# Value products by halves of the context rows, in a fused cross-attention and expert kernel

## The chip, the cores and the metric

The kernel runs on one core of a Trainium2 chip. A core has a matrix engine (TensorE, PE in the profile, with its weight loads shown apart as PEld), a vector engine (VectorE, DVE), an engine for activation functions (ScalarE, ACT), a general one (GpSimd, POOL) and an engine that only issues transfers (SyncE, SP). Transfers can be put on queues by SyncE, ScalarE and GpSimd. The time is device microseconds for one execution, as the median of several runs; the profile is one further execution, recorded by the hardware profiler.

## The reference

Inputs are x (8 batches of 512 tokens, 256 wide), a condition vector per batch, a context of 64 rows per batch, and weights. All is float32.

```python
nx = _layer_norm(x, ln_gamma, ln_beta)
q = nx @ Wq
k = prototype_bank @ Wk            # the context
v = prototype_bank @ Wv
scores = jnp.einsum('bth,bph->btp', q, k) * H ** (-0.5)
weights = jax.nn.softmax(scores, axis=-1)
evidence = jnp.einsum('btp,bph->bth', weights, v)
anchor = jnp.broadcast_to(global_anchor[:, None, :], nx.shape)   # the condition
combined = jnp.concatenate([nx, evidence, anchor], axis=-1)
router_probs = jax.nn.softmax(combined @ router_W + router_b, axis=-1)
h = jax.nn.silu(jnp.einsum('btc,ecr->bter', combined, e_w1) + e_b1)   # 3 experts
expert_out = jnp.einsum('bter,erh->bteh', h, e_w2) + e_b2
routed = jnp.sum(expert_out * router_probs[..., None], axis=-2)
g = jax.nn.sigmoid(jax.nn.silu(combined @ gate_w1 + gate_b1) @ gate_w2 + gate_b2)
return x + g * (routed @ out_w + out_b)
```

## The kernel before

The eight batches are worked in four pairs. One long opening prepares what all pairs need and the first pair's own inputs; then a loop over the pairs runs a gate layer, three expert layers and the outputs. The instructions are written out by hand in one order, and each engine works through its own part of that order; nothing is reordered between engines but by waits on data.

The opening, from line 1200 on, is what the change touches. The context (512 rows in all) arrives in two halves of 256 rows on SyncE's queue, then Wv and the first two batches of x; Wk and Wq arrive on ScalarE's queue. `wake` (line 289) runs products of a tile of zeros on PE into a bank that nothing reads: seven ahead of the first data and one between the two context halves (each product is two instructions in the trace[...]). `context_transposes` (line 311) turns each half on PE and copies it to `ctxT`, the first half by VectorE, the second by ScalarE. `transpose_weights` (326) turns Wk and Wq. `project` (335) with Wv makes the values, 128 of their columns at a time over all 512 context rows, and `keep_v` (344) copies them. `join_keys` (347) multiplies the two weight matrices into one, so that scores can be had from the context and the normalised x without separate keys and queries; `project` with that product and `keep_m` (358) give `mr`, in which the first context row of each batch is subtracted from the others.

Beside this VectorE computes `statistics` (540) and `normalize` (553) of both batches, with the square root on ScalarE in `deviation` (550); `transpose_x` (574) turns the result on PE, and `scale_x` (564) applies scale and shift, one half of the width on VectorE and one on ScalarE. `small_transposes` (297) turns the rows of biases and the condition.

`scores` (642) multiplies, and starts the softmax on VectorE; for the first pair it subtracts the largest score on VectorE and leaves the exponential to one instruction on ScalarE. `value_weights` (762) multiplies values by expert weights, `value_differences` (782) prepares one part of the result. `softmax` (686) and `turn_weights` (692) finish the attention weights.

The first layers use a scheme with seven products in place of eight for a two-by-two block product. `combine_x` (631) makes the four differences t1 to t4 of x that it needs, in the tile T and in two parts of the second batch's x; `nx_product` (843) uses them. In the first pair's case t1 and t2 are computed ahead of `scores`, t3 behind the softmax, and t4 in the first expert layer.

PSUM banks of the opening are taken in rotation by `either` (283). The rotation is one line:

```python
        return bank((1, 2, 0, 3)[turn[0] % 4], name)
```

Of the kernel before, what the change touches and what calls it, by code (L numbers as in the profile page):

```python
# [10 lines left out]
ALU = mybir.AluOpType  # L11
# [5 lines left out]
def kernel(  # L17
# [100 lines left out]
    def load_table(func):  # L118
        nc.scalar.activation(warm_t, warm_t, func)
# [32 lines left out]
    def rows_of(w):  # L152
        return w.rearrange("(k p) n -> p k n", p=P)
# [8 lines left out]
    def by_k(flat, n):  # L162
# [14 lines left out]
    rw, rw2, m0, rw_all, gamma_all = (  # L177
        scr[:, NL : NL + 3 * KH * E].rearrange("p (k e) -> p k e", e=E),
        scr[:, NL + P : NL + P + KH * TB].rearrange("p (k e) -> p k e", e=TB),
        scr[:, NL + 2 * P : NL + 2 * P + B],  # L180
        scr[:, NL + 4 * P : NL + 4 * P + H * E].rearrange("p (d e) -> p d e", e=E),
        scr[:, NL + 4 * P + H * E : NL + 4 * P + H * E + H],
    )
# [105 lines left out]
    def wake(n):  # L289

        if not ps_wake:
            ps_wake.append(misc("ps_wake"))
        for _ in range(n):
            nc.tensor.matmul(ps_wake[0][:, :P], zeros, zeros, start=True, stop=True)  # L294


    def small_transposes():
        pt = either("pt_rows")
        nc.tensor.transpose(pt[:, :NR], rows, ident[:NR, :NR])
        nc.vector.tensor_copy(cols, pt[:, :NR])  # L300
        nc.gpsimd.tensor_copy(b2T[:, :, :E], b2_c.rearrange("p e k -> p k e"))
        pt = either("pt_cond")
        for k in range(KH):
            nc.tensor.transpose(
                pt[:, k * B : (k + 1) * B], cond_sb[:, k * P : (k + 1) * P], ident[:B, :B]
            )
        nc.vector.tensor_copy(
            condT[:, :, :B], pt[:, : KH * B].rearrange("p (k b) -> p k b", b=B)
        )

    def context_transposes():
        for d in range(2):
            if d:
                wake(1)
            pt = either(f"pt_ctx_{d}").rearrange("p (k c) -> p k c", k=KH)
            for k in range(KH):
                for t in range(NX // 2):
                    nc.tensor.transpose(
                        pt[:, k, t * P : (t + 1) * P],
                        ctx_sb[:, d * (NX // 2) + t, k * P : (k + 1) * P],  # L320
                        ident,
                    )
            half = slice(d * NX // 2 * P, (d + 1) * NX // 2 * P)
            (nc.scalar.copy if d else nc.vector.tensor_copy)(ctxT[:, :, half], pt)

    def transpose_weights(dst, w_sb, name):
        pt = either(f"pt_{name}")
# [13 lines left out]
                )  # L341
            evacuate(m, ps)

    def keep_v(m, ps):
        nc.scalar.copy(vT[:, m, :], ps)

    def join_keys():

        ps = either("ps_kq").rearrange("p (m n) -> p m n", n=H)
        for m in range(KH):  # L350
            for k in range(KH):
                nc.tensor.matmul(
                    ps[:, m, :], wkT[:, k, m * P : (m + 1) * P], wqT[:, k, :],
                    start=(k == 0), stop=(k == KH - 1),
                )
        nc.scalar.copy(wkqT, ps)

    def keep_m(m, ps):
        ps = ps.rearrange("p (b c) -> p b c", c=CT)
        nc.vector.tensor_copy(m0, ps[:, :, 0])  # L360
        nc.vector.tensor_tensor(
            mr[:, m, :, 1:], ps[:, :, 1:], m0.unsqueeze(2).to_broadcast([P, B, CT - 1]), ALU.subtract
        )


# [208 lines left out]
    def transpose_x(b):  # L574
        S["nxT", b] = npool.tile([P, KH, T], F32, tag="nxT", name=f"nxT_{b}")
        for k in range(KH):
            pt = misc(f"pt_x_{b}_{k}")
            for t in range(NT):
                nc.tensor.transpose(
                    pt[:, t * P : (t + 1) * P], S["xn", b][:, t, k * P : (k + 1) * P], ident  # L580
                )
            scale_x(S["nxT", b][:, k, :], k, pt, k % 2 == 0)

    def logits(j):

# [45 lines left out]
    def combine_x(j, engine, ts=range(4)):  # L631

        b11, b21, b12, b22 = (S["nxT", 2 * j + i][:, k, :] for i in range(2) for k in range(KH))
        if 0 in ts:
            S["T", j] = work.tile([P, 3, T], F32, tag="T", name=f"T_{j}", bufs=1)
        t1, t2, t4 = (S["T", j][:, i, :] for i in range(3))
        t3 = b12
        for i, (dst, p, q) in enumerate(((t1, b12, b11), (t2, b22, t1), (t3, b22, b12), (t4, b21, t2))):
            if i in ts:
                engine.tensor_tensor(dst, p, q, ALU.subtract)  # L640

    def scores(j):


        ps = misc(f"ps_s_{j}")
        for g in range(2):
            for k in range(KH):
                for i, h in SIDES:
                    nc.tensor.matmul(  # L649
                        ps[side(i, h), g * NH : (g + 1) * NH],  # L650
                        mr[:, k, 2 * j + i, g * TB : (g + 1) * TB],
                        S["nxT", 2 * j + i][:, k, h * NH : (h + 1) * NH],
                        start=(k == 0),
                        stop=(k == KH - 1),
                    )
        w = work.tile([P, 2, NJ, TB], F32, tag="w", name=f"w_{j}", bufs=1)
        S["w", j] = w
        tokens = w.rearrange("p g j c -> p j g c")
        nc.vector.transpose(w.rearrange("p g j c -> p (g j c)"), ps)
        nc.vector.tensor_copy(logits(j)[:, 1, :], w[:, 0, :, 0])  # L660
        nc.vector.memset(w[:, 0, :, 0], 0.0)
        mx = work.tile([P, NJ], F32, tag="mx", name=f"mx_{j}")
        nc.vector.tensor_reduce(mx, tokens, AX.XY, ALU.max)
        sm = work.tile([P, NJ], F32, tag="sm", name=f"sm_{j}")
        S["sm", j] = sm
        if j == 0:
            nc.vector.tensor_tensor(w, w, by_token(mx), ALU.subtract)
            nc.scalar.activation(w, w, AF.Exp, scale=SCALE)
            return
        nmx = work.tile([P, NJ], F32, tag="nmx", name=f"nmx_{j}")  # L670
        nc.vector.tensor_scalar_mul(nmx, mx, -SCALE)
        for t in range(NJ):
            nc.scalar.activation(
                w[:, :, t, :], w[:, :, t, :], AF.Exp, bias=nmx[:, t : t + 1], scale=SCALE,
                accum_out=sm[:, t : t + 1],
            )
# [6 lines left out]
    def by_token(a):  # L683
        return a.unsqueeze(1).unsqueeze(3).to_broadcast([P, 2, NJ, TB])
# [158 lines left out]
    def nx_product(j, n, which, start=False):  # L843
        q = GROUPS[n]
        c = 2 * q
        A, Bx, T_ = S["nxT", 2 * j], S["nxT", 2 * j + 1], S["T", j]

        def a(k, d):
            return w1[:, k, (c + d) * P : (c + d + 1) * P]

        dst, lhsT, rhs = {
            1: (U, a(0, 0), A[:, 0, :]),
            2: (Y, a(1, 0), A[:, 1, :]),
            3: (Z, ws[:, S4, q, :], Bx[:, 1, :]),
            4: (U, a(1, 1), T_[:, 2, :]),
            5: (Z, ws[:, S1, q, :], T_[:, 0, :]),
            6: (U, ws[:, S2, q, :], T_[:, 1, :]),
            7: (U, a(0, 1), Bx[:, 0, :]),
        }[which]
        product(dst[n], lhsT, rhs, start=start)  # L860

# [337 lines left out]

    with tc.manual_schedule(engines=None):  # L1200
        ctx_rows = context.flatten_outer_dims().rearrange("(t p) d -> p t d", p=P)
        for d in range(2):
            half = slice(d * NX // 2, (d + 1) * NX // 2)
            nc.sync.dma_start(ctx_sb[:, half, :], ctx_rows[:, half, :])
        for w_sb, w in ((wk_sb, Wk), (wq_sb, Wq)):
            nc.scalar.dma_start(w_sb, rows_of(w))
        nc.sync.dma_start(wv_sb, rows_of(Wv))
        load_table(AF.Sqrt)
        load_x(0)
        load_x(1)  # L1210
# [4 lines left out]
            load_first(g)  # L1215

        wake(7)
        context_transposes()
        transpose_weights(wkT, wk_sb, "wk")
        transpose_weights(wqT, wq_sb, "wq")  # L1220
        statistics(0, 0, NT)
        deviation(0, 0)
        normalize(0)
        project(wv_sb, ctxT, keep_v, "v", (0,))
        join_keys()
        project(wv_sb, ctxT, keep_v, "v", (1,))
        statistics(1, 0, NT // 2)
        small_transposes()
        statistics(1, NT // 2, NT)
        transpose_x(0)  # L1230
        deviation(0, 1)
        load_router_column()
        normalize(1)
        load_table(AF.Exp)
        project(wkqT, ctxT, keep_m, "m")
        router_anchor()
        transpose_x(1)
        value_weights(0, E)
        store_router_rows(0)
        store_router_anchor()  # L1240
        combine_weights(E)
        combine_x(0, nc.vector, (0, 1))
        scores(0)
        router_column()
        spread_router_bias()
        combine_weights(0)
        spread_router_rows(0)
        value_weights(0, 0, nc.scalar.copy, False)
        anchor_rows(E)
        anchor_rows(0)  # L1250
        sum_weights(0)
        softmax(0)
        value_differences(0, 0)
        combine_x(0, nc.vector, (2,))
        turn_weights(0)
        late_scratch()
        load_anchor(1)
# [123 lines left out]
```

## Time and profile before

| | us |
|---|---|
| median of 3 runs | 462.98 (462.89 to 463.24) |
| the profiled execution | 463.12 |
| its span, first to last instruction | 461.3 |
| PE busy in the span | 456.4 |
| VectorE busy | 365.2 |
| ScalarE busy | 214.7 |
| GpSimd busy | 100.4 |

The opening lasts until about 24.4 us, when the first gate product begins. A line of the chain gives the start, the length and the work of a piece that the end of the program hangs on. A line of the timeline gives start, length, engine, line in the kernel, operation, output and inputs, and in brackets how long the engine had been idle and what ended that. The durations of single PE instructions overlap, because they are pipelined; the distance from one start to the next tells the rate.

### The profile page before, as it was taken

What the parts mean: (1) busy time and instruction counts of PE and PEld (TensorE: products, weight loads), DVE (VectorE), ACT (ScalarE), POOL (GpSimd) and SP (SyncE); (2) the same over time, 40 slices, a digit from 0 to 9 for tenths busy, and PEclk for the clock granted to TensorE, in tenths of its full rate; (3) what the DMA queues carried; (4) which work ended last, traced back from release to release, by engine and by line L of the source; (5) the groups of instructions that cost most, each with busy time, mean ns of one, the idle gap of its engine ahead of it and who ended that gap; (6) DMA issues with size and microseconds to landing.
All of it is one profiled execution on the core that took longest, in us unless ns stands there. A gap on an engine that the chain in (4) does not pass through costs nothing.

```text
span 461.3 us, 4752 instructions
## 1 busy us (share of the span) xinstructions
PE 456.4 (99%) x1455; PEld 210.1 (46%) x1455; DVE 365.2 (79%) x683; ACT 214.7 (47%) x370; POOL 100.4 (22%) x149
## 2 busy tenths in 40 slices
PE   9999999999999999999999999999999999999996
PEld 7544555444444444444444444444444444444445
DVE  2988979969799669869799659879889625787973
ACT  3445683664222666556221576548221456457000
POOL 6357715001181200001072300001072300000020
PEclk9999999999999999999999999999999999999999
DMA  8975677302013326802012235702011570000013
GB/s 275 370 158 128 102 232 126 83 0 46 7 23 46 76 87 142 159 18 46 6 24 32 37 136 120 110 0 46 6 24 23 82 195 0 0 0 1 0 22 70
DMA packets 119401, 35.27 MB, mean 76 GB/s; under 512 B 106044, under 2 KB 116336, under 8 KB 118864
## 3 DMA queue, kind: packets, MB, share of 16 engines
q1 hardware_dynamic: 115312, 27.02, 28.9%
q0 software_dynamic: 2176, 7.17, 4.7%
q10 hardware_dynamic: 1888, 0.79, 0.6%
q8 instruction: 11, 0.18, 0.2%
q14 instruction: 14, 0.11, 0.1%
HBM read 27.56 MB, written 7.39 MB: 76 GB/s over the span
## 4 chain that ended last, share of the span: by engine, by line
PE 95%; DVE 4%; issue 0%
PE ps_u L796 43%; PE ps_z L796 18%; PE ps_y L796 14%; PE ps_vw L771 5%; PE ps_gu L796 3%; PE ps_w2o L501 2%; PE ps_s L649 2%; PE ps_gz L796 1%; DVE h L1072 1%; PE ps_tokens L796 1%; PE ps_wake L294 1%; DVE h L880 1%; PE ps_v L339 1%; PE ps_m L339 1%; PE ps_gy L796 1%; DVE r L1082 0%
## 5 line engine op out<-in xcount | busy, mean ns | idle before, releaser
L880 DVE TENSOR_TENSOR h<-h,pb 128x512 f32<-128x512 f32 x96 | 61.9, 694 | 6.5 <-ACT h L829 6.5
L796 PE MATMUL ps_u<-h,w2o 128*128 128x512 f32 x144 | 64.2, 595 | 0.0
L829 ACT ACTIVATE h<-h,abias 128x512 f32<-128x512 f32 x72 | 49.6, 719 | 13.5 <-DVE h L835 13.0
L796 PE MATMUL ps_u<-nxT,w 128*128 128x512 f32 x112 | 55.3, 604 | 0.0
L796 PE MATMUL ps_z<-wT,vw 64*128 64x512 f32 x104 | 49.5, 605 | 0.0
L1105 POOL TENSOR_TENSOR yb<-yb,xb 128x512 f32<-128x512 f32 x14 | 17.8, 1269 | 142.9 <-DVE yb L1104 138.8
L796 PE MATMUL ps_z<-h,w2s 128*128 128x512 f32 x96 | 42.6, 593 | 0.2 <-DVE r L1088 0.2
L796 PEld LDWEIGHTS ps_u<-h,w2o 128*128 128x128 f32 x144 | 27.0, 190 | 32.7 <-issue 29.4
L838 ACT COPY h<-ps_u 128x512 f32<-128x512 f32 x48 | 28.0, 582 | 29.4 <-PE ps_u L796 26.9
L415 POOL DMA_DIRECT2D vrd<-vw x8 | 5.0, 630 | 136.9 <-ACT vw L778 136.9
L1072 DVE TENSOR_TENSOR h<-h,h 128x1024 f32<-128x1024 f32 x24 | 34.3, 1483 | 0.0
L796 PEld LDWEIGHTS ps_u<-nxT,w 128*128 128x128 f32 x112 | 20.2, 189 | 29.5 <-issue 24.2
L829 ACT ACTIVATE h<-ps_u,abias 128x512 f32<-128x512 f32 x24 | 16.5, 688 | 29.7 <-PE ps_z L796 29.4
L796 PEld LDWEIGHTS ps_z<-h,w2s 128*128 128x128 f32 x96 | 18.1, 190 | 23.5 <-issue 21.8
L796 PE MATMUL ps_y<-nxT,w 128*128 128x512 f32 x56 | 28.6, 592 | 0.0
L796 PE MATMUL ps_z<-T,ws 128*128 128x512 f32 x56 | 28.6, 592 | 0.0
L835 DVE TENSOR_TENSOR h<-h,ps_y 128x512 f32<-128x512 f32 x24 | 16.4, 683 | 14.8 <-PE ps_y L796 14.0
L796 PE MATMUL ps_u<-wT,vw 64*128 64x512 f32 x56 | 27.8, 611 | 0.0
L796 PE MATMUL ps_y<-wT,vw 64*128 64x512 f32 x56 | 27.0, 596 | 0.0
L771 PE MATMUL ps_vw<-w,vT 128*128 128x512 f32 (+1 forms) x64 | 26.9, 542 | 0.0
L796 PE MATMUL ps_u<-T,ws 128*128 128x512 f32 x56 | 26.6, 592 | 0.0
L796 PE MATMUL ps_u<-T,w 128*128 128x512 f32 x56 | 26.6, 592 | 0.0
(229 smaller groups left out, 792.2 us busy)
## 6 DMA issues: line engine op xcount, KB each, us to landing
pb<-pd POOLq DMA_DIRECT2D x4, 1536.0 KB, 6.5
xb<-in_x_dram SPq DMA_DIRECT2D x64, 64.0 KB, 2.4
out_dram<-yb SPq DMA_DIRECT2D x56, 64.0 KB, 2.0
w<-in_L_xcond_e_w_dram SPq DMA_DIRECT2D x6, 512.0 KB, 10.1
x<-in_x_dram SPq DMA_DIRECT2D x24, 128.0 KB, 2.9
xd<-x SPq DMA_DIRECT2D x24, 128.0 KB, 2.4
xg<-xd SPq DMA_DIRECT2D x48, 64.0 KB, 2.4
scr_wa<-in_L_xcond_e_w_dram SPq DMA_DIRECT2D x3, 512.0 KB, 16.5
```

What stands on the lines that cost most here:

```text
L339: nc.tensor.matmul(ps, w_sb[:, k, m * P : (m + 1) * P], src[:, k, :], start=(k == 0), stop=(k == KH - 1))
L415: nc.gpsimd.dma_start(S["vrd", j][i].rearrange("e c -> c e"), S["vw", j][row_half(i), R0:])
L501: nc.tensor.matmul(ps[:, d * H : (d + 1) * H], w2T[:, k, (i + d) * P : (i + d + 1) * P], ow_sb[:, k, :], start=(k == 0), stop=(k == KH - 1),)
L649: nc.tensor.matmul(ps[side(i, h), g * NH : (g + 1) * NH], mr[:, k, 2 * j + i, g * TB : (g + 1) * TB], S["nxT", 2 * j + i][:, k, h * NH : ( ...
L771: nc.tensor.matmul(ps, vT[:, k, j * 2 * CT : (j + 1) * 2 * CT], w1[:, KH + k, n0:n1], start=(k == 0), stop=(k == KH - 1),)
L796: nc.tensor.matmul(ps, lhsT, rhs, start=start, stop=True, skip_group_check=not start)
L829: nc.scalar.activation(h, h if src is None else src, AF.Silu, bias=abias[:, c, 2 * j + i : 2 * j + i + 1])
L835: nc.vector.tensor_tensor(h, h, part, ALU.add)
L838: nc.scalar.copy(chunk(n, i, d), part)
L880: nc.vector.tensor_tensor(h, h, S["pb", j][:, i, :, 2 * q // RC, :], ALU.mult)
L1072: nc.vector.tensor_tensor(d, p, m, ALU.subtract)
L1105: nc.gpsimd.tensor_tensor(yb, yb, S["xb", 2 * j + row][:, i, :], ALU.add)
```

## The change

The context halves and Wv are each loaded in two pieces of 128 KB, one on SyncE's queue and one on ScalarE's; Wk and Wq move to SyncE's queue, behind them. Values are computed by halves of the context rows: `values(0)` as soon as the first half is turned, with three products of `wake` between, and `values(1)` ahead of `join_keys`. The two copies of a context half are shared by VectorE and ScalarE. The copy of the key product is made in two parts. The copies of the small transposes, the first column of `mr`, and the k = 0 half of the first batch's x go from VectorE to ScalarE. The products for `mr` stand around `transpose_x(0)`, and their subtractions come after the second batch is normalised. The table of the exponential is loaded later. In the first pair t3 and t4 change places, t3 is computed with t1 and t2, and the value products of the first expert and their difference are placed around the exponential.

```diff
-        scr[:, NL + 2 * P : NL + 2 * P + B],
+        scr[:, NL + 2 * P : NL + 2 * P + KH * B].rearrange("p (m b) -> p m b", b=B),
...
-        nc.vector.tensor_copy(cols, pt[:, :NR])
+        nc.scalar.copy(cols, pt[:, :NR])
...
-        nc.vector.tensor_copy(
-            condT[:, :, :B], pt[:, : KH * B].rearrange("p (k b) -> p k b", b=B)
-        )
-
-    def context_transposes():
-        for d in range(2):
-            if d:
-                wake(1)
+        nc.scalar.copy(condT[:, :, :B], pt[:, : KH * B].rearrange("p (k b) -> p k b", b=B))
+
+    def context_transposes(*ds):
+        for d in ds:
...
-            (nc.scalar.copy if d else nc.vector.tensor_copy)(ctxT[:, :, half], pt)
+            nc.vector.tensor_copy(ctxT[:, 0, half], pt[:, 0, :])
+            nc.scalar.copy(ctxT[:, 1, half], pt[:, 1, :])
...
-    def keep_v(m, ps):
-        nc.scalar.copy(vT[:, m, :], ps)
+    def values(d):
+
+        half = slice(d * NX // 2 * P, (d + 1) * NX // 2 * P)
+        ps = either(f"ps_v_{d}").rearrange("p (m c) -> p m c", m=KH)
+        for m in range(KH):
+            for k in range(KH):
+                nc.tensor.matmul(
+                    ps[:, m, :], wv_sb[:, k, m * P : (m + 1) * P], ctxT[:, k, half],
+                    start=(k == 0), stop=(k == KH - 1),
+                )
+        nc.scalar.copy(vT[:, :, half], ps)
...
-        nc.scalar.copy(wkqT, ps)
-
-    def keep_m(m, ps):
-        ps = ps.rearrange("p (b c) -> p b c", c=CT)
-        nc.vector.tensor_copy(m0, ps[:, :, 0])
+            nc.scalar.copy(wkqT[:, m, :], ps[:, m, :])
+
+    def first_column(m, ps):
+        products[m] = ps.rearrange("p (b c) -> p b c", c=CT)
+        nc.scalar.copy(m0[:, m, :], products[m][:, :, 0])
+
+    products = {}
+
+    def keep_m(m):
+        ps = products.pop(m)
         nc.vector.tensor_tensor(
-            mr[:, m, :, 1:], ps[:, :, 1:], m0.unsqueeze(2).to_broadcast([P, B, CT - 1]), ALU.subtract
+            mr[:, m, :, 1:], ps[:, :, 1:], m0[:, m, :].unsqueeze(2).to_broadcast([P, B, CT - 1]), ALU.subtract
         )
...
-            scale_x(S["nxT", b][:, k, :], k, pt, k % 2 == 0)
+            scale_x(S["nxT", b][:, k, :], k, pt, k % 2 == 0 and b > 0)
...
         t3 = b12
+        if j == 0:
+            t3, t4 = t4, t3
...
             nc.vector.tensor_tensor(w, w, by_token(mx), ALU.subtract)
+            value_weights(0, 0, nc.scalar.copy, False)
             nc.scalar.activation(w, w, AF.Exp, scale=SCALE)
+            value_differences(0, 0)
             return
...
-        for d in range(2):
-            half = slice(d * NX // 2, (d + 1) * NX // 2)
-            nc.sync.dma_start(ctx_sb[:, half, :], ctx_rows[:, half, :])
-        for w_sb, w in ((wk_sb, Wk), (wq_sb, Wq)):
-            nc.scalar.dma_start(w_sb, rows_of(w))
-        nc.sync.dma_start(wv_sb, rows_of(Wv))
+        halves = [slice(d * NX // 2, (d + 1) * NX // 2) for d in range(2)]
+        for dst, src in (
+            (ctx_sb[:, halves[0], :], ctx_rows[:, halves[0], :]),
+            (wv_sb, rows_of(Wv)),
+            (ctx_sb[:, halves[1], :], ctx_rows[:, halves[1], :]),
+        ):
+            for k, queue in enumerate((nc.sync, nc.scalar)):
+                queue.dma_start(dst[:, k : k + 1, :], src[:, k : k + 1, :])
+        nc.sync.dma_start(wk_sb, rows_of(Wk))
+        nc.sync.dma_start(wq_sb, rows_of(Wq))
...
         wake(7)
-        context_transposes()
+        context_transposes(0)
+        wake(3)
+        values(0)
+        context_transposes(1)
         transpose_weights(wkT, wk_sb, "wk")
         transpose_weights(wqT, wq_sb, "wq")
         statistics(0, 0, NT)
         deviation(0, 0)
         normalize(0)
-        project(wv_sb, ctxT, keep_v, "v", (0,))
+        values(1)
         join_keys()
-        project(wv_sb, ctxT, keep_v, "v", (1,))
         statistics(1, 0, NT // 2)
         small_transposes()
         statistics(1, NT // 2, NT)
+        project(wkqT, ctxT, first_column, "m", (0,))
+        deviation(0, 1)
         transpose_x(0)
-        deviation(0, 1)
         load_router_column()
         normalize(1)
-        load_table(AF.Exp)
-        project(wkqT, ctxT, keep_m, "m")
+        project(wkqT, ctxT, first_column, "m", (1,))
+        for m in range(KH):
+            keep_m(m)
         router_anchor()
         transpose_x(1)
         value_weights(0, E)
+        load_table(AF.Exp)
         store_router_rows(0)
         store_router_anchor()
         combine_weights(E)
-        combine_x(0, nc.vector, (0, 1))
+        combine_x(0, nc.vector, (0, 1, 2))
         scores(0)
         router_column()
         spread_router_bias()
         combine_weights(0)
         spread_router_rows(0)
-        value_weights(0, 0, nc.scalar.copy, False)
         anchor_rows(E)
         anchor_rows(0)
         sum_weights(0)
         softmax(0)
-        value_differences(0, 0)
-        combine_x(0, nc.vector, (2,))
         turn_weights(0)
```

## The prediction

> **What bounds the kernel now.** I read the page's busy shares first, then the chain of work that ended last, in order of time for the opening 33 us, then the timeline of the same stretch. The first says who is full.
>
> ```profile
> span 461.3 us, 4752 instructions
> PE 456.4 (99%) x1455; PEld 210.1 (46%) x1455; DVE 365.2 (79%) x683; ACT 214.7 (47%) x370; POOL 100.4 (22%) x149
> PE 95%; DVE 4%; issue 0%
> ```
>
> TensorE (PE) is busy 99% and holds 95% of the chain. A busy PE can hide slow or waiting matmuls, so the chain of the opening is needed. Its columns are start, length, and piece.
>
> ```profile
> 1.06 3.35 PE ps_wake L294 x14
> 4.41 1.03 PE pt_ctx L318 x4
> 5.44 0.43 PE ps_wake L294 x2
> 5.86 1.03 PE pt_ctx L318 x4
> 6.90 0.44 PE pt_wk L330 x4
> 7.33 0.44 PE pt_wq L330 x4
> 7.77 1.79 PE ps_v L339 x4
> 9.56 1.73 PE ps_kq L352 x8
> 11.28 1.72 PE ps_v L339 x4
> 13.00 0.17 PE pt_rows L299
> 13.17 0.11 PE pt_cond L304 x2
> 13.28 1.02 PE pt_x L579 x8
> 14.30 3.44 PE ps_m L339 x8
> 17.74 0.18 PE ps_rb L377 x4
> ```
>
> Two things are to be seen. Four transposes cost 1.03 us until 6.9 us and 0.44 us after it: two wakes in 0.43 us are 0.215 us each, four transposes in 0.44 us are 0.11 us each. PE works at half speed until about 6.8 us. (The granted clock in the rows of a window reads 1.00 throughout here, so the spacing must tell it.) And from 6.9 us on the pieces join: 0.22 us per 256 columns, 0.43 us per 512, apart from 0.05 to 0.15 us where a transpose follows a matmul or the reverse. The only waits for data are before 6.9 us: each pt_ctx takes 1.03 us where four at 0.215 us are 0.86 us, so 0.17 us twice, until the two context halves land at about 4.24 and 5.70 us (issue at 0.7 and 1.2 us, landing 3.5 and 4.5 us later). The timeline shows what the other engines do.
>
> ```profile
> 5.78 0.72 PEld L318 LDWEIGHTS pt_ctx<-ident,scr_ctx 128*128 128x128 f32 x4 [0.21 <-DMA scr_ctx<-in_ctx_dram]
> 8.61 0.43 DVE L547 BATCH_NORM_STATS2 st<-x 128x6 f32<-128x256 f32 x1 [2.44 <-DMA x<-in_x_dram]
> 15.92 1.38 DVE L559 TENSOR_SCALAR x<-x,mv,rstd 128x256 f32<-128x256 f32 x4
> 24.82 0.63 ACT L668 ACTIVATE w<-w 128x512 f32<-128x512 f32 x1 [4.50 <-DVE w L667]
> ```
>
> VectorE (DVE) waits for x to 8.6 us, then normalises both batches just ahead of PE; ScalarE (ACT) has gaps of microseconds. PE therefore ends when its work is done: a change before 33 us is worth only what it alters in PE's own work, in the slow stretch, or in a wait that reaches PE.
>
> **The change, PE first.** I put the after-order on the chain's clock. The 14 wakes still end at 4.41 us. First context half: four transposes at 0.215 us are 0.86 us; with the old wait 1.03 us; I take 0.95, since half the bytes now lie ahead of it but part comes over ScalarE's queue. That ends at 5.36. wake(3) in place of wake(1): six instructions at 0.215 us, 1.29 us, to 6.65. values(0): eight matmuls of 256 columns, the form of ps_kq, 1.73 us at full speed. The clock changed at 6.9 on this scale; if it does so again, 0.25 us run slowly and do 0.125 us of work, so 0.25 + 1.605 = 1.86 us, to 8.51. The second half's transposes, now at full speed, cost 0.44 us and about 0.14 us for the switch (eight pt_x take 1.02 us where 0.88 is due), to 9.09. pt_wk and pt_wq 0.88, to 9.97. values(1) 1.73 + 0.07 switch (the first ps_v is 1.79, the second 1.72), to 11.77. join_keys 1.73, to 13.50. Before, this point was 13.00: **+0.50 us**. The parts: four more wake instructions and a switch more, less the waits that fall away at half their length. Then rows, condition, m0, transpose_x(0), m1: the same pieces in another order, with one switch more, **+0.07 us**. Together +0.57 us.
>
> **Copies, with their cover.** The two ctxT copies (DVE 0.69 us, ACT 0.59 us) become four of 128x256. The nearest rows are ACT's 0.38 us for 128x258 and DVE's 0.41 us on 128x256, run side by side. The first pair ends near 6.0 us, under the wakes that last to 6.65; with no wakes PE would wait about 0.6 us there. The second pair is done near 9.7 us even behind the 0.58 us copy of values(0) on ACT, and values(1) starts at 9.97. The key product's copy becomes two of 0.38 us (0.76 for 0.59, ACT): the first lies under join_keys' second half; the second, done near 14.1 us, is wanted by m0's second half at about 14.7, and pt_rows and pt_cond lie between. Without that cover PE would wait 0.5 us. The cols and condT copies (0.15 and 0.17 us on DVE) go to ACT, where the nearest small row is 0.27 us; they are wanted at transpose_x(0)'s scaling near 16 us. first_column goes to ACT (0.16 us on DVE, 0.2 to 0.3 there). The scaling of the first x's k = 0 half goes from DVE (0.79 us) to ACT (0.78 us). ACT then has about 2 us more between 12 and 20 us, where it showed 5.5 us busy in ten.
>
> **Waits that the order adds.** DVE now has the second context copy ahead of its statistics. That copy can start when PE ends the transposes, about 9.2 us, not at 6.9; so statistics(0) starts near 9.6 us instead of 8.61. Behind it wait deviation(0,0), ACT's copy of values(1), normalize(0), and so on. Statistics and normalising of x0 took 4.2 us (8.61 to 12.79): done at 13.8, wanted at transpose_x(0) near 15.6. Statistics(1) end near 15.9 (four times 0.53, with the two small copies gone). deviation(0,1) sits on ACT behind first_column(0), which waits for m0's end at 15.5; it finishes near 16.2. normalize(1) needs 0.2 + 1.4 us, done at 17.9; transpose_x(1) wants it at about 18.6. Cover left: 0.7 us. Then the two subtractions of keep_m (0.68 us each) and the scaling of 0.80 us on DVE end near 20.2 us; scores wants them at 19.91 + 0.57 = 20.5 us. Cover left: 0.3 us. I cost both at nothing.
>
> **Loads.** ScalarE issues three pieces instead of Wk and Wq, SyncE five before x0 instead of three; at 0.46 us an issue x0 goes out near 3.1 us instead of 2.24. The bytes ahead of x0 are 1.28 MB either way, and the engines move 340 to 380 GB/s from 3 us on, so I leave x0's landing at 8.6 us. Here a rule of the Trainium skill speaks against the change: "DMA: Bandwidth & Descriptors", section "Rules for kernel authors", says that splitting a transfer or spreading it over issuing engines brings no bandwidth, since all use the same 16 engines. The row: ScalarE's Wk and SyncE's first context half, both issued at 0.74 us, landed after 3.9 and 3.5 us, sharing the engines. By the rule the first half gains only the order of its bytes: at most the 0.17 us wait, about 0.09 on the path at half speed. If the split brought the halves at twice the pace, it would be no more, because the 14 wakes end at 4.41 anyway. Both give about the same sum. Wv is wanted at 6.65, Wk at 9.1, Wq at 9.5; the old landings were 6.9 for Wv, 4.6 for Wk, 6.2 for Wq. Wv moves from behind 1 MB to behind 256 KB, so I put it near 4.7 us. Cover 1.9 us.
>
> **The softmax part.** The third difference of x, the value copy, value_differences and the Exp table are moved to where DVE or ACT had gaps; that lets wT come about 1 us earlier on DVE. PE did not wait there: its first evidence products at 31.5 us are spaced like those of the next three rounds (0.09 us over plain, each time). The gain on the path is nothing, between 0 and 0.1 us. SyncE's later loads and POOL's stores keep their order; POOL's router store waits for a copy about 0.4 us later, with over 1.5 us until PE wants its sums.
>
> **Sum.** +0.57 us, rounded to +0.5 for the possible 0.1. The profiled execution took 463.12 us: its span of 461.3 and 1.8 around it; so it becomes 463.6. The median before is 462.98, 0.14 lower; I forecast **463.5 us**, +0.11%. About 0.2%, 0.93 us, is what a measurement of this kernel can tell from no change: below 462.05 is faster, above 463.91 slower.
>
> **Rivals.** (1) *The clock comes up earlier.* For it: the slow stretch held a wait twice and eight transposes, and "TensorE: Matmul & The Clock Gate", section "Part 4: PE-mode transpose", says that transposes don't count as PE activity for the gate; now matmuls stand there. Against: four transposes came just before the change at 6.8 us and it came all the same. The same page's warm-up of 3.4 us of activity would put it at 4.5 us; the row says 5.7 us after the first wake. With 4.5, the opening from 4.4 to 6.8 us runs at double speed but waits for the copies: values(0) from about 5.5, everything 1.1 us sooner, 463.5 - 1.1 = **462.4 us**. Even that is no 0.2%.
> (2) *The late statistics reach PE (slower).* Place: DVE's copy ahead of statistics(0), through deviation(0,1) and normalize(1) to transpose_x(1) and scores. It costs PE whatever exceeds the 0.3 to 0.7 us of cover; it decides for slower at 0.4 us beyond it, thus 1.1 us of added lateness. x0 landing 1 to 2 us later behind SyncE's two more loads, or ACT's longer queue (each small copy at 0.3 us), could do it: 463.5 + 0.8 = **464.3 us**.
> (3) *The two-queue loads don't deliver.* A piece on ScalarE's queue lands late: its first packets came about 1 us after SyncE's. A late context piece costs half its lateness (slow clock), a late Wv beyond 6.65 all of it: **464.1 us** for 0.6 us.
>
> **How the numbers follow.** The likeliest case has 0.60 (its own range 463.1 to 464.0: 0.52 of it within 0.2%, 0.08 slower). Rival 1: 0.14 (0.09 same, 0.05 faster). Rival 2: 0.16 (0.13 slower, 0.03 same). Rival 3: 0.10 (0.06 slower, 0.04 same). Sums: faster 0.05, same 0.68, slower 0.27. The range leaves out a tenth on each side: 462.4, where rival 1 ends, to 464.4, just past rival 2.
>
> **What would show it.** Right: the chain is joined from 5 us on, pt_wk starts near 9.1, pt_rows near 13.5, scores near 20.5, evidence near 32.0, all about half a microsecond late, and the rest of the span is the same. Rival 1: pieces at double speed before 6 us. Rival 2: a weight load of pt_x or ps_s waiting for DVE. Rival 3: ps_v waiting for a DMA. The forecast is wrong if any wait over 0.4 us stands on PE behind 6.9 us, or if the clock steps up at another time than about 6.8 us.

## The result, and the profile after

The median went from 462.97 us (462.75 to 463.49, 22 runs) to **463.96 us** (463.31 to 466.35, 22 runs): ratio 1.0025, 95% interval 1.0019 to 1.0032. The change costs 1.0 us. The forecast was 463.5 us, in the range 462.4 to 464.4. The profiled execution took 463.63 us, 0.51 more than that of before. Nineteen of the 22 runs lie between 463.31 and 464.70. The other three (465.9 to 466.4) show a mean granted clock of 0.996 where all others show 0.999 or 1.0; 0.004 of 463 us is 1.85 us, about their excess.

The page of the changed kernel shows the busy shares as before, and one difference in the chain:

```profile
PE 455.8 (99%) x1467; PEld 210.7 (46%) x1467; DVE 364.8 (79%) x679; ACT 216.3 (47%) x377; POOL 100.6 (22%) x149
PE 93%; DVE 4%; DMA 2%; ACT 0%; issue 0%
```

PE is still 99% busy, but the chain has moved 2% from PE to a DMA. The chain of work in order of time (start, length, piece) says which:

```profile
3.40 5.46 DMA x<-in_x_dram
...
11.15 0.30 ACT sd L562
11.44 0.47 ACT vT L351
11.92 0.28 ACT scr_k L362
...
12.24 1.13 PE ps_kq L358 x4
13.38 0.17 PE pt_rows L299
...
31.97 0.62 PE ps_y L811
```

Before, the chain of this stretch was PE from end to end. Now it runs through the load of x0 (issued at 3.40 us, landed at 8.86), its statistics, and three instructions of ScalarE, and comes back to PE in the middle of `join_keys`. The timeline of the same execution shows it from PE's side (start, length, engine, line, operation; in brackets the idle time and what ended it):

```profile
4.08 0.60 PE L314 MATMUL pt_ctx<-ident,scr_ctx 128*128 128x128 f32 x4
...
4.71 0.42 DVE L320 COPY scr_ctx<-pt_ctx 128x256 f32<-128x256 f32 x1 [3.69 <-PE pt_ctx L314]
5.17 0.37 ACT L321 COPY scr_ctx<-pt_ctx 128x256 f32<-128x256 f32 x1 [1.53 <-DVE scr_ctx L320]
...
8.33 1.89 PE L347 MATMUL ps_v<-scr_ctx,scr_w 128*128 128x256 f32 x8
...
10.06 1.03 PE L358 MATMUL ps_kq<-scr_w,scr_k 128*128 128x256 f32 x4
...
12.24 1.13 PE L358 MATMUL ps_kq<-scr_w,scr_k 128*128 128x256 f32 x4 [1.16 <-ACT scr_k L362]
```

Three things are to be seen.

**A wait inside the key product.** The second four matmuls of `join_keys` could follow the first at 10.06 + 0.88 = 10.94 us. They start at 12.24, because they wait for ScalarE's copy of the first four. That copy needs only the first four, but it stands on ScalarE behind deviation(0,0), which waits for x0, and behind the copy of values(1).

**The context copies are not side by side.** ScalarE's begins at 5.17 us, when VectorE's of the same bank has ended.

The Trainium skill has a rule that would account for both, and the prediction did not look it up: "PSUM — Partial Sum Buffer", section "PSUM bank collisions raise a hardware error", says that two engines must not touch one PSUM bank (in the same quarter of partitions) at once, reads beside reads included, and that the compiler puts a dependency between any two instructions that would. The trace agrees that there is such a dependency: 0.42 us of VectorE before ScalarE starts, 1.16 us of idle PE that ScalarE's copy ends. By the rule the first part of a split copy can't lie under the second half of the product, since in the kernel both halves are parts of one bank (`ps` of `join_keys`). Who put the dependency into this program, and what would happen without it, no run here shows.

**The clock came up early.** values(1) starts at 8.33 us where the ledger had 9.97. The first four transposes, at 4.08 us, were busy for 0.60 us; in the kernel before the same four, from 4.35 us on, were busy for 1.09. So PE gained 1.6 us on the forecast's opening, and the wait in `join_keys` took it back: the pieces behind it stand at 13.38, 20.33 and 31.97 us, near the forecast's 13.5, 20.5 and 32.0. In this execution the size came out by two errors that cancel.

### The profile page after: what moved, and what is told of

The parts are those of the page before. It is cut to its first block, busy times and chain, and to the rows that moved or that the text cites. A ratio compares the mean times of both kernels' runs of the same rounds, so it can differ in the third digit from the quotient of the medians.

```text
span 461.6 us, 4784 instructions
## 1 busy us (share of the span) xinstructions
PE 455.8 (99%) x1467; PEld 210.7 (46%) x1467; DVE 364.8 (79%) x679; ACT 216.3 (47%) x377; POOL 100.6 (22%) x149
## 4 chain that ended last, share of the span: by engine, by line
PE 93%; DVE 4%; DMA 2%; ACT 0%; issue 0%
PE ps_u L811 43%; PE ps_z L811 18%; PE ps_y L811 14%; PE ps_vw L786 5%; PE ps_gu L811 3%; PE ps_w2o L512 2%; PE ps_s L662 2%; PE ps_gz L811 1%; DVE h L1090 1%; DMA x<-in_x_dram 1%; PE ps_tokens L811 1%; PE ps_m L336 1%; DVE h L898 1%; PE ps_gy L811 1%; DMA scr_ctx<-in_ctx_dram 1%; DVE r L1100 0%
## 5 line engine op out<-in xcount | busy, mean ns | idle before, releaser
L811 PE MATMUL ps_z<-nxT,ws 128*128 128x512 f32 x56 | 26.6, 592 | 0.0
```

Source lines behind the costliest of these rows:

```text
L811: nc.tensor.matmul(ps, lhsT, rhs, start=start, stop=True, skip_group_check=not start)
```

## The experiments

**The split copy, joined again (one part undone), and moved past x0 (the cause of its lateness taken away).** In the first, the key product is copied whole, after both halves. In the second the copy stays split, but deviation(0,0) and normalize(0) come behind its first part.

```diff
# e1, against the changed kernel
-            nc.scalar.copy(wkqT[:, m, :], ps[:, m, :])
+        nc.scalar.copy(wkqT, ps)
# e2, against the changed kernel
             nc.scalar.copy(wkqT[:, m, :], ps[:, m, :])
+            if m == 0:
+                deviation(0, 0)
+                normalize(0)
...
-        deviation(0, 0)
-        normalize(0)
         values(1)
```

> The changed kernel with the copy of the key product made whole again, after both halves of join_keys. Theory A (PE's second half of join_keys waits for ScalarE's copy of the first half, and that copy stands behind deviation(0,0), which waits for statistics of x): the wait of 1.3 us inside ps_kq goes; a shorter one comes ahead of the first ps_m, because the whole copy still ends near 12.5 us. PE is about 1.0 us earlier at ps_m; 463.0 us, the spread of the runs shrinks. Theory B (x normalised too late reaches PE at transpose_x(1) or scores, the copy is harmless): the wait moves there, 464.0 us as now.

> The changed kernel with the copy still in two parts, but deviation(0,0) and normalize(0) put between them, so that the first part no longer stands behind the wait for x. Theory A: the second half of join_keys still waits for the copy's own length, about 0.55 us in place of 1.3; 463.2 us. Theory B: no change or slower, 464.0 us or more, since normalize(0) is 0.25 us later.

The whole copy: 463.56 us (17 runs; 463.10 before on the same chip), ratio 1.0010 (1.0002 to 1.0017). Deviation behind the copy: 463.63 us (12 runs), 1.0011 (1.0003 to 1.0020). Against the kernel before on the same chip the changed kernel is 0.99 us longer, these two 0.46 and 0.53: either takes back about half. Both stay above the 463.0 and 463.2 us that theory A expected. The chain of the second shows what is left of the wait when ScalarE has nothing in front of the copy:

```profile
10.40 0.88 PE ps_kq L358 x4
11.30 0.38 ACT scr_k L362
11.72 1.13 PE ps_kq L358 x4
```

The eight matmuls take 2.45 us (10.40 to 12.85) where unbroken they take 1.73: a split copy costs PE 0.72 us even with ScalarE free, the copy of 0.38, its hand-over, and a slower start of PE (1.13 us for four matmuls where the first four took 0.88). The whole copy is no cure either. In its profiled execution, at 464.55 us one of its two slowest, x0 landed at 11.02 us, and PE waited one step later:

```profile
3.68 7.34 DMA x<-in_x_dram
...
14.62 1.98 PE ps_m L336 x4
```

The copy still stands behind deviation(0,0) on ScalarE (13.31 to 13.61 us here), now with the m product waiting for it.

**The split alone, in the kernel before; and x0 made later.** The first does one part of the change alone. The second loads x1 ahead of x0 in the changed kernel.

```diff
# e3, against the kernel before
-        nc.scalar.copy(wkqT, ps)
+            nc.scalar.copy(wkqT[:, m, :], ps[:, m, :])
# e4, against the changed kernel
-        load_x(0)
         load_x(1)
+        load_x(0)
```

> The kernel before with one edit: the copy of the key product in two parts. Theory A: PE stops between the halves of join_keys from about 10.3 to 12.0 us, since there too ScalarE's copy stands behind deviation(0,0), and a copy of values besides: 1.8 us slower, 464.8 us. Theory B: no change, 463.0 us.

> The changed kernel with the load of the second batch of x put ahead of the first one, so that x0 lands 512 KB later, about 1.4 us at 370 GB/s. Theory A: statistics(0), deviation(0,0) and the copy are later by the same amount, the wait inside ps_kq grows from 1.3 to about 2.7 us: 465.3 us. Theory B: the wait appears at transpose_x instead and is shorter, since statistics of both batches end at the same time: 464 to 464.5 us.

The split alone: 465.64 us (4 runs), 1.0056 (1.0041 to 1.0072). Two and a half microseconds for one line, in a kernel whose loads are as they were. x1 first: 467.10 us (4 runs), 1.0096 (1.0066 to 1.0125). Theory A expected 464.8 and 465.3 us, and the profiled executions agree: 464.88 and 465.70. What the medians have beyond that goes with the clock: two of the other runs of the first, and all three others of the second, show a mean granted clock of 0.993 to 0.996, and they are the longest. The chain of the first:

```profile
2.24 6.27 DMA x<-in_x_dram
...
11.89 1.13 PE ps_kq L352 x4
```

and of the second:

```profile
3.87 7.19 DMA x<-in_x_dram
...
14.45 1.13 PE ps_kq L358 x4
```

From the landing of x0 to the second half of the key product it is 12.24 - 8.86 = 3.38 us in the changed kernel, 11.89 - 8.51 = 3.38 here, and 14.45 - 11.06 = 3.39 with x1 first. The same distance three times, with x0 landing at three times: where the wait binds, PE's time is x0's landing plus a constant. That is shown.

**The loads: whole transfers, and the new loads alone in the kernel before.** In the first, the context halves (SyncE) and Wv (ScalarE) are one transfer each. The second keeps the kernel before, but with the change's loads. The third is the first with the whole key copy.

```diff
# e5, against the changed kernel (e7: and the edit of e1)
...
+        for queue, dst, src in (
+            (nc.sync, ctx_sb[:, halves[0], :], ctx_rows[:, halves[0], :]),
+            (nc.scalar, wv_sb, rows_of(Wv)),
+            (nc.sync, ctx_sb[:, halves[1], :], ctx_rows[:, halves[1], :]),
         ):
-            for k, queue in enumerate((nc.sync, nc.scalar)):
-                queue.dma_start(dst[:, k : k + 1, :], src[:, k : k + 1, :])
+            queue.dma_start(dst, src)
# e6, against the kernel before: the changed kernel's loads
...
-        for w_sb, w in ((wk_sb, Wk), (wq_sb, Wq)):
-            nc.scalar.dma_start(w_sb, rows_of(w))
-        nc.sync.dma_start(wv_sb, rows_of(Wv))
...
+            for k, queue in enumerate((nc.sync, nc.scalar)):
+                queue.dma_start(dst[:, k : k + 1, :], src[:, k : k + 1, :])
+        nc.sync.dma_start(wk_sb, rows_of(Wk))
+        nc.sync.dma_start(wq_sb, rows_of(Wq))
```

> The changed kernel with the same order of loads, but the context halves and Wv each as one transfer (first half on SyncE, Wv on ScalarE, second half on SyncE). Theory C (the pieces on two queues leave part of each later transfer behind: in the profiles of the changed loads the last sixteenth of x0 landed 0.6 to 2.7 us after half of it, before 0.2 us): x0 lands near 8.6 us in every execution, the runs above 465 us vanish, the wait inside ps_kq stays at about 1.2 us: 463.7 us, all runs within 0.6 us. Without C: the same median and spread as the changed kernel, 463.3 to 466.

> The kernel before with the loads of the change alone. Theory C: x0 lands 0.5 to 2.5 us later than 8.6, of which 0.4 us are covered at transpose_x(0), while the context is there 1 us sooner and helps before that: 463.3 to 465 us with a spread over 1 us. Without C: 462.7 to 463.0 us, as narrow as the kernel before.

> The changed kernel with both undone: transfers whole as in the run above, and the copy of the key product whole. Theories A and C together: no wait inside ps_kq, a short one of 0.3 to 0.5 us ahead of ps_m, no late x0: 462.9 us, all runs within 0.6 us, so level with the kernel before. If the rest of the change costs something of its own, as the prediction's sum of added wakes and switches has it, 463.4 us.

Whole loads: 464.56 us (6 runs), 1.0040 (1.0026 to 1.0055). Whole loads with the whole copy: 463.68 (16 runs), 1.0013 (1.0006 to 1.0020), level with the whole copy alone. So undoing the pieces gains nothing, and the thought that they make x0 late falls: x0 landed at 9.14 us in the first and 9.64 in the other, later than with pieces (8.86). The chain of e5 is worth showing, since in it the clock came up at about 6.4 us and PE sets the pace but for the one copy, nearly as the forecast had assumed (its key product takes 2.46 us, from 11.37 to pt_rows, against 1.73 unbroken):

```profile
6.60 1.73 PE ps_v L347 x8
...
8.77 0.44 PE pt_wk L327 x4
...
11.37 0.88 PE ps_kq L358 x4
...
13.83 0.17 PE pt_rows L299
```

And in the chain of e7 the key product is unbroken, but its whole copy has nothing to hide under: `join_keys` now comes last.

```profile
11.20 1.74 PE ps_kq L358 x8
...
13.61 1.98 PE ps_m L336 x4
```

From 12.94 to 13.61 us PE waits but for the two small transposes, which take 0.28. In the kernel before, the second product for the values stood there, 1.72 us.

The new loads in the kernel before: 463.67 us (9 runs), 1.0022 (1.0012 to 1.0031). Its chain shows a price that the change's own order of work hides: Wk, landed at 4.66 us before, lands at 7.34, and PE's first transposes of it start at 7.38 instead of 6.90.

```profile
2.12 5.22 DMA scr_w<-in_L_xcond_Wk_dram
```

That is the time which theory C expected of this run, though e5 and e7 speak against the theory's cause. In its profile x0 landed at 9.72 us, and that too reached PE, by way of VectorE, at a place that the forecast had named: `scores` starts at 20.99 us after a wait of 0.25 us for VectorE's scaling.

**The key copy with cover.** This has the whole copy, and puts half of values(1) behind `join_keys`, where the kernel before had a product too.

```diff
# e10, against the changed kernel, with the edit of e1
...
-        values(1)
+        values(1, [0])
         join_keys()
+        values(1, [1])
```

> The changed kernel with the copy of the key product whole and values(1) divided: half of its products ahead of join_keys, half behind it, so that 0.86 us of PE work lie between the key product and its use. Theory E (also a whole copy is not hidden where values(1) stands ahead of join_keys; the kernel before hid it behind its second product of values): the wait of 0.4 to 0.7 us ahead of ps_m goes, 463.1 us against 463.6 with the whole copy alone. Without E: 463.6 us.

463.39 us (13 runs; 462.97 before), 1.0006 (0.9998 to 1.0014): the lowest of the kernels with values by halves, and not told from no change. Its chain has no wait behind the key product, but a new one ahead of it:

```profile
10.15 0.50 ACT scr_w L330
...
10.69 1.99 PE ps_kq L358 x8
...
13.55 0.17 PE pt_rows L299
```

The key product needs ScalarE's two copies of the turned weights (0.59 and 0.60 us), and these stand behind its copies of values(0) and of the second context half. The whole of values(1) had covered them; half of it does not. From values(1)'s first half at 9.50 us to its second at 12.52 it is 3.02 us, where the products themselves take 0.86 + 1.73: 0.43 us are lost. The clock came up at about 6.6 us in this execution. That pt_rows stands at 13.55 us, beside the ledger's 13.50, is therefore not the ledger come true: the steps ahead of this wait ran some 0.4 us sooner than forecast, as in e5, and the wait took it back.

**The weights on ScalarE's queue.** Wk and Wq go out on ScalarE, behind its pieces, so that SyncE reaches x sooner; once in the changed kernel, once in e10.

```diff
# e9, against the changed kernel; e12, against e10
-        nc.sync.dma_start(wk_sb, rows_of(Wk))
-        nc.sync.dma_start(wq_sb, rows_of(Wq))
+        nc.scalar.dma_start(wk_sb, rows_of(Wk))
+        nc.scalar.dma_start(wq_sb, rows_of(Wq))
```

> The changed kernel with Wk and Wq back on ScalarE's queue, behind its three pieces. Theory D (what makes the end of x0's transfer late is that SyncE's queue alone carries Wk and Wq ahead of x0; the pieces have nothing to do with it): the last of x0 lands within 0.3 us of its half, near 8.5 us, the runs above 465 us vanish; the wait inside ps_kq and the clock's step remain: 463.7 us. Without D: as the changed kernel, 464.0 us with single runs near 466.

> Both edits: values(1) around join_keys with the whole copy, and Wk and Wq on ScalarE's queue. Theories D and E: 462.9 us, level with the kernel before, no run above 464. If the late context copies or the clock's step set the opening, 463.3 us.

Both missed by far: 468.35 us (4 runs), 1.0125 (1.0109 to 1.0140), and 468.24 us (5 runs), 1.0115 (1.0101 to 1.0130). The chain of e9 says why:

```profile
3.56 8.60 DMA scr_w<-in_L_xcond_Wq_dram
...
12.30 0.63 PE pt_wq L327 x4
```

Wq went out only at 3.56 us, beside both batches of x that SyncE had sent at 2.12 and 3.37, and landed at 12.16; in the changed kernel it had landed by 7.4. PE was idle 2.6 us for it. x0, sent 1.3 us sooner than in the changed kernel, landed later (9.60). In the profile of e12 the wait had a second price. A window's line gives the stretch and its length, the busy times, and, behind POOL's, the granted clock, then two figures of the DMA:

```profile
11.00:14.50 3.50, 2.02 (x7) 1.87 (x8) 0.67 (x4) 0.78 (x2) 0.96 (x6) 0.52 1.07 336
14.50:18.00 3.50, 3.50 (x9) 2.75 (x9) 3.33 (x13) 0.37 (x1) 0.00 (x0) 0.50 1.05 386
```

Within the idle stretch the clock fell, and PE ran at half speed until 18 us. In the profile of e9, with nearly the same wait, it did not (1.00 in both windows). That profile is e9's fastest run, though: its other three, and all five of e12, show a mean granted clock of 0.993 to 0.996.

**The softmax part alone, and a gentler change of the kernel before.** The first makes only the change's moves around the softmax: the third difference with the first two, t3 and t4 exchanged, the value products around the exponential. The second keeps the order of the kernel before. It loads context half 0 and Wk on SyncE and context half 1 and Wq on ScalarE, then Wv, and moves the small copies and x0's k = 0 scaling to ScalarE.

```diff
# e11, against the kernel before
+        if j == 0:
+            t3, t4 = t4, t3
...
-        combine_x(0, nc.vector, (0, 1))
+        combine_x(0, nc.vector, (0, 1, 2))
...
# e8, against the kernel before
...
-        for d in range(2):
+        for d, queue in enumerate((nc.sync, nc.scalar)):
...
-        for w_sb, w in ((wk_sb, Wk), (wq_sb, Wq)):
-            nc.scalar.dma_start(w_sb, rows_of(w))
+        nc.sync.dma_start(wk_sb, rows_of(Wk))
+        nc.scalar.dma_start(wq_sb, rows_of(Wq))
```

> The kernel before with only the part around scores and softmax: t3 with t1 and t2, t3 and t4 in each other's place, value products and their difference around the exponential. The prediction's statement that this is worth nothing on the path: 463.0 us, between -0.1 and 0; from the trace of the changed kernel, where the product with t4 starts 0.15 us later, +0.15 us: 463.2. If wT was on the path: 462.5 us.

> The kernel before with three edits: the context halves as whole transfers on two queues ahead of the weights, the small copies of cols and condT on ScalarE, and the scaling of the first x wholly on ScalarE. PE has the context about 1 us sooner, and VectorE, which feeds scores just in time, 1.1 us less to do: 462.6 us. If VectorE's feeding or the clock's step takes the gain back, 463.0 us as before.

The softmax part: 463.05 us (13 runs), 1.0001 (0.9993 to 1.0009), nothing. The gentler change: 462.82 us (13 runs; 463.03 before), 0.9997 (0.9989 to 1.0005). It is the lowest median of all, and can't be told from the kernel before. No kernel run here beats that one for certain.

## Why the prediction was right, and where it was not

The sign, the size within half a microsecond and the place (all of it in the opening) were right. The steps behind them fared unevenly, and that the number fell well inside the range is in part luck: with the stop of the copy put in, the ledger would have said +1.3 us, and in the profiled execution an early clock, which the ledger did not have, gave back what the copy took.

**The step that failed: the split copy.** "The key product's copy becomes two of 0.38 us …: the first lies under join_keys' second half." It did not; the second half waits for it. Sized by e2 and e5 that is +0.72 us where x0 is in time, which by itself takes the ledger from +0.57 to about +1.3. Where x0 is late it is whatever puts the second half at x0's landing plus 3.38 us. The prediction even said what would refute it, "any wait over 0.4 us … on PE behind 6.9 us"; there is one of 1.16 us.

**The clock.** "If it does so again" at 6.9 us: it need not. By the spacing of PE's instructions the step came at 6.8 us in the profile of before, 3.9 in the changed kernel, and anywhere from 4.0 to 7.2 us in the profiles of the experiments. Up to 3.9 us PE does the same in before and after: the same wakes. In the Trainium skill, "TensorE: Matmul & The Clock Gate", section "Part 1: The HAM clock gate", calls the window free-running, of about 3.4 us, so that the step depends on where in it the first matmul falls. The steps here spread over 3.3 us, about one such window, which agrees; that the page puts the variation at half a microsecond either way does not fit these runs. The prediction weighed that page's rule on transposes for rival 1, and not this one. Rival 1 did happen in the profiled execution, 1.6 us of it, and was swallowed by the wait.

**The loads** (landings by the last of a transfer's sixteen completion steps in the trace). The first context half landed at 3.38 us instead of 4.21. The order of bytes alone would account for most of that: the 256 KB of Wk, which came beside it before, take 0.7 us at the 340 to 380 GB/s that the prediction read (an estimate). Whether the pieces also started faster (0.41 MB had come by 3.2 us, against 0.23 before) was not tested. PE had no use for it, as forecast, since the wakes lasted to 4.1 us. Wv landed at 4.37 (forecast 4.7), Wk and Wq before they were wanted: rival 3 falls in this execution. (Its ground was misread besides: in the kernel before, ScalarE's first packets came at 2.35 us, half a microsecond after SyncE's at 1.81, not one.) x0 was put at 8.6 us and landed at 8.86 in the profile, at 9.0 to 11.0 in those of e1, e2, e5, e7 and e10. Its issue was put at 3.1 us and came at 3.40: the chain shows it waiting for the first context piece. In the kernel before, x0 left at 2.24 us.

**Rival 2** had the right mechanism, late statistics that reach PE by way of deviation, at the wrong place. It named deviation(0,1) and `transpose_x(1)`, with 0.3 to 0.7 us of cover. That cover held: the second batch's normalising ends at 17.6 us, and its transposes start at 18.36. The statistics reached PE 6 us sooner, through deviation(0,0) and the copy behind it on ScalarE.

**The rest of the ledger** stands. e5 gives its pieces one by one: values(0) at 6.60 us (forecast 6.65), pt_wk at 8.77 (9.09), join_keys at 11.37 (11.77), where about 0.13 us of the lead are the earlier clock, and most of the rest is the two switches (0.14 and 0.07 us) that the ledger charged and this chain does not show. The moves around the softmax are worth nothing (e11). One small term was missed: the first expert's product with t4 started about 0.15 us late in the profile, as VectorE's subtraction for it, 1.10 us from 35.40 on, was then still running.

**Where the 1.0 us of the medians goes.** Each kernel is taken against the kernel before on its own chip: 0.99 us for the changed kernel, 0.46 for e1, 0.65 for e7, 0.42 for e10. Joining the copy takes back about half a microsecond; that is shown. The missing cover of the whole copy (e1 and e7 against e10) comes to 0.0 to 0.2 us, no more than medians can tell here, and e10 pays for it with another wait. What is left, some 0.4 us for the added wakes and the order of work, is argued: e10's interval does not exclude nothing.

That the changed kernel's runs spread over 1.4 us where the old ones spread over 0.7 fits the same reading. The old opening waits for its second context half, which lands at 5.74 us: with the clock up at 4.2 instead of 6.8 us (the profile of e3), its first product for the values starts at 7.03 instead of 7.61. In the new order values(1) starts at 8.3 to 8.5 us with the clock up at 3.9 to 4.3 (changed kernel, e2), and at 9.6 to 9.8 with the clock up at 6.7 to 7.2 (e4, e1). That the spread of the runs comes from this is argued, not shown.

What stays open is why x0 lands late. Cutting transfers in pieces is not it (e5, e7), and sending x0 sooner is no cure (e9). The landings from the second context half on have a tail: half of a transfer's sixteen steps are in, and the last follows 0.6 to 2.7 us later for x0 (0.2 to 0.5 in before, e3 and e8).

## What to carry to other kernels

Before a copy out of PSUM is split to start earlier, ask whether the product goes on in the same bank: in this program each part was then a stop for PE (0.7 us) and not an overlap. Ask as well what stands ahead of it on its own in-order engine: a square root that waits for a load 5 us long became PE's wait. And when a product is moved, look for the copies that it used to cover: moving half of one back (e10) laid another copy bare.

## What the runs showed that was not expected

**Eight transfers at a time.** SyncE's and ScalarE's loads share eight semaphores in this program, and from the ninth on an issue waits for the earlier transfer whose semaphore it takes over. In the kernel before, the ninth load waits for Wk (what waits and for what; us in total, times, longest):

```profile
SPq L223 <- DMA scr_w<-in_L_xcond_Wk_dram: 0.8, 1, 0.8
```

Wk landed at 4.66 us and the load went out at 4.67, though the first context half had been there since 4.21. In the changed kernel the ninth load is x0, which the pieces pushed back to that place: it waits for ScalarE's first context piece (landed at 3.38, issue at 3.40). In e9 Wq is the tenth and waits for the same piece (3.54 and 3.56). So a load cut in two also uses up two of the eight places.

**What a wait of PE costs besides.** In e12's profile two waits, of 1.2 and 2.8 us, were followed by half clock until 18 us; 6.8 us at half clock cost 3.4 us of work, which is that execution's mean clock of 0.993. By the same sum 0.996 is some 3.7 us at half clock (an estimate). Runs at 0.996 or less are 3 of 22 in the changed kernel, 2 of 4 in e3, 3 of 4 in e4 and in e9, all 5 in e12, and 1 each in e5 and e6. There are none among the 58 of e1, e2, e7 and e10, in whose profiles no wait of PE in the opening reaches 1 us, and none in the kernel before. This suggests that the longer waits bring the clock down, but in the profiles of e5 and e6 no wait is over 0.6 us. Only e12's profile shows the fall itself.

The same 256 KB of Wq took 4.8 us from issue to landing behind the context on SyncE's queue, and 8.6 us on ScalarE's beside both batches of x.
